# Row transfers in pairs behind a slot's adds, outputs written over fetched rows, and q . bk by ScalarE

## The chip, the cores and the metric

The kernel runs on one core of a Trainium2 chip. The metric is device time in microseconds of one execution; lower is better. Engines are named as in the profile: PE (TensorE), DVE (VectorE), ACT (ScalarE), POOL (GpSimd, which also issues the indirect DMAs) and SP (SyncE, which issues most direct DMAs). Each engine works through its own instructions strictly in order, and waits for others on semaphores.

## The reference

The input is an image batch x of 4 x 256 channels x 64 x 64, in float32. Two layers follow each other.

```python
# layer 0: group norm, then attention over a 3x3 window of every pixel, added to x
x = x + L0_conv(gn(x), Wq, bq, Wk, bk, Wv, bv, Wo, bo)
#   q = (xn @ Wq + bq) * scale; k, v over the padded image; softmax over 9 neighbours; out @ Wo + bo
# layer 1: pixels become 4 x 4096 tokens of 256 values
t = tokens(x)
t = t + L1_attn(ln(t), Wp, bp, Wg)     # gate g = sigmoid(tanh(t Wp + bp) Wg); windowed sum of g*t over 64, divided by that of g
t = t + L1_ffn(ln(t), router_w, w1, b1, w2, b2)
#   out = tokens + sum over the 2 best of 8 experts of weight * (gelu(tokens @ w1[e] + b1[e]) @ w2[e] + b2[e])
x = from_tokens(t)
```

In the last step each of the 16,384 tokens goes through two of eight experts only. The kernel uses that: it sorts token rows by expert, runs each expert on its own rows, and adds the results back to the tokens.

## The kernel before, in words

**Blocks.** The 16,384 pixels are cut into 32 blocks g of 512 (eight per image), and a block into four tiles of 128 tokens. Four generators work on a block, one after the other, each in a later round of the main loop: `produce(g)` normalises x and computes v and q (L455, L459, L481, L485); `attend(g)` makes the 3x3 attention (L535 to L577) and the first token norm, whose reciprocal root is L339 on POOL; `tail(g)` does the gated window sum, stores the token sum to `out` (L685), and leaves the normalised rows in a tile `tok` with each token's eight expert weights and its row number behind the 256 values; `ranks(g)` counts, with two small matmuls, at which row of which expert's region each token stands (`rows`, cast by DVE at L768). In round g of the loop `attend(g)`, `ranks(g - 2)`, `tail(g - 1)` and `produce(g + 1)` take turns.

**Row transfers.** At the end of `ranks` a block's rows are written to HBM (`rows_in`) sorted by expert: four tiles by two choices, so eight indirect DMAs of 128 rows per block, 256 in all, issued by POOL (L783). The helper `paced` makes each wait for the latest marked ACT instruction, so that they are spread out. The inner function `dispatch` declares that transfers don't depend on each other, and records them for the fetches.

**Slots.** A slot is 256 rows of one expert. There are 135. They are grouped: thirteen groups of two blocks, then six of one block (`GROUPS`), and a group's slots can be fetched when all transfers of its blocks have landed. Groups have 1, then twelve times 8, five times 4 and at last 18 slots. For slot m the generator `experts()` emits: `fetch` (SP, L882: 256 rows into a tile sx of the pool `rowp`, of seven buffers), `matrix` (ACT, L899) and `pixels` (PE transposes L906, ACT copy L910) two slots ahead of the output; `hidden` (PE L918, ACT gelu L924) one slot ahead; `output` (PE L936, then DVE L940 adds b2 into a tile ys of three buffers and L941 multiplies by the token's weight), for each of two halves of 128 rows; and `add` one slot behind. A fetch is emitted two slots ahead of its `pixels`, so four ahead of the slot's output.

**Adds.** `add` issues two indirect DMAs on POOL (L954) that add the 128 rows of ys each to `out`, with the row numbers taken from sx. Two slots may add to the same token, so both wait until both adds of the slot before have landed. The first slot of a group also waits for the stores of its blocks.

**Order.** The functions are written in this order, and a scheduler places the instructions of each engine; what is decided once is fixed in the engine's program. `follow` emits slots at an even pace between `knots`, so that the slots of one group run while the blocks of the next are produced. What is left of the slots after the last block runs alone.

**The sums q . bk.** For each block three small POOL instructions (L468, L471, L474) add the constant `qbk` to one column of v and leave `qdotb`, which the softmax of the next round needs (L547).

Of the kernel before, what the change touches and what calls it, by code (L numbers as in the profile page):

```python
# [46 lines left out]
FP = mybir.dt.float32  # L47
AF = mybir.ActivationFunctionType
ALU = mybir.AluOpType
# [3 lines left out]
P = 128  # L53
# [9 lines left out]
def hybrid_block_kernel(ctx: ExitStack, tc: tile.TileContext, ins: dict, out: bass.AP):  # L63
    nc = tc.nc
    x = ins["x"]
    B, C, HW = x.shape
    W = 64
    NC = C // P
    TB = 512
    NT = TB // P  # L70
# [11 lines left out]
    FETCH = 2  # L82
    I32, U32 = mybir.dt.int32, mybir.dt.uint32
    ENG = mybir.EngineType
    GROUPS = (*[2] * 13, *[1] * 6)
    assert sum(GROUPS) == NB
    where = [(k, j) for k, n in enumerate(GROUPS) for j in range(n)]

    U = 2
# [10 lines left out]
    RW = C + 2 * E  # L100
    IN_RANGE = "a slot's expert and row are computed on the chip from counts of a known sum"

    const = ctx.enter_context(tc.tile_pool(name="const", bufs=1))
    xsp = ctx.enter_context(tc.tile_pool(name="xsp", bufs=4))
    xp = ctx.enter_context(tc.tile_pool(name="xp", bufs=XBUFS))
    xtp = ctx.enter_context(tc.tile_pool(name="xtp", bufs=TBUFS))
    vp = ctx.enter_context(tc.tile_pool(name="vp", bufs=3))
# [1 line left out]
    w2p = ctx.enter_context(tc.tile_pool(name="w2p", bufs=2))  # L109
    w3p = ctx.enter_context(tc.tile_pool(name="w3p", bufs=3))  # L110
    w4p = ctx.enter_context(tc.tile_pool(name="w4p", bufs=4))
    slotp = ctx.enter_context(tc.tile_pool(name="slotp", bufs=3))
    rowp = ctx.enter_context(tc.tile_pool(name="rowp", bufs=FETCH + 5))
    w1sp = ctx.enter_context(tc.tile_pool(name="w1sp", bufs=3))
    hbm = ctx.enter_context(tc.tile_pool(name="hbm", bufs=1, space=bass.MemoryType.DRAM))
    ps_a = ctx.enter_context(tc.tile_pool(name="ps_a", bufs=5, space=PSUM))
# [243 lines left out]
    qb = const.tile([P, NC], FP, tag="qb", name="qb")  # L360
    vo = const.tile([P, NC, C + 1], FP, tag="vo", name="vo")
    qbk = const.tile([P, 1], FP, tag="qbk", name="qbk")
    bqb = w2p.tile([P, 2, NC, P], FP, tag="xl_tok", name="bqb")
    for ci in range(NC):
        nc.gpsimd.tensor_copy(bqb[:, 0, ci, :], bq[:, ci : ci + 1].to_broadcast([P, P]))
        nc.gpsimd.tensor_copy(bqb[:, 1, ci, :], bv[:, ci : ci + 1].to_broadcast([P, P]))
# [59 lines left out]
    def produce(g):  # L426
        if g >= NB:
            return
        b, i = divmod(g, NBI)
        if i == 0:  # L430
            image_norm(b)
        mean, rc = norm[b]
        t = xn[g] = xt.pop(g)
        lo = W if i == 0 else 0
        hi = XW - W if i == NBI - 1 else XW
        for c in range(NC):
            tc.keep_in_program_order(nc.vector.tensor_scalar(  # L437
                t[:, c, lo:hi], t[:, c, lo:hi], mean[:, c : c + 1], rc[:, c : c + 1],
                ALU.subtract, ALU.mult,
            ))  # L440
        if lo:
            nc.gpsimd.memset(t[:, :, 0:lo], 0.0)
        if hi < XW:
            nc.gpsimd.memset(t[:, :, hi:XW], 0.0)
        yield


        v = vp.tile([P, NT, C + 1], FP, tag="v", name=f"v_{g}")
        vt[g] = v
        if i == 0:  # L450
            v0[b] = w1p.tile([P, C + 1], FP, tag="v0", name=f"v0_{b}")
        for j in range(0 if i == 0 else 1, NT + 1):
# [12 lines left out]
        qdotb = w2p.tile([P, NT], FP, tag="qdotb", name=f"qdotb_{g}")  # L465
        ct[g] = qdotb
        H = P // 2
        nc.gpsimd.tensor_scalar(  # L468
            qdotb[0:H, 0:1], first[H:P, C : C + 1], qbk[H:P], None, ALU.add
        )  # L470
        nc.gpsimd.tensor_scalar(  # L471
            qdotb[0:H, 1:NT], v[H:P, 0 : NT - 1, C], qbk[H:P], None, ALU.add
        )
        nc.gpsimd.tensor_scalar(qdotb[H:P, :], v[0:H, :, C], qbk[0:H], None, ALU.add)  # L474

        q = w2p.tile([P, NC, TB], FP, tag="q", name=f"q_{g}")
        qt[g] = q
        for co in range(NC):
            ps = ps_a.tile([P, TB], FP, tag="a", name=f"psq_{g}_{co}")
            for ci in range(NC):  # L480
                nc.tensor.matmul(  # L481
                    ps, qk[:, ci, co * P : (co + 1) * P], t[:, ci, W : W + TB],
                    start=(ci == 0), stop=(ci == NC - 1),
                )
            nc.scalar.activation(q[:, co, :], ps, AF.Identity, bias=qb[:, co : co + 1])  # L485
            if co == NC - 1:

                tc.keep_in_program_order(nc.vector.tensor_add(
                    xT[g], xT[g], outb.unsqueeze(1).to_broadcast([P, NT, C])
                ))  # L490
            yield
# [99 lines left out]
    def tail(g):  # L591
# [73 lines left out]
            if t == 1:  # L665
                yield
        mv, rstd = token_norm([t2[:, t, :] for t in range(NT)], f"f{g}", rsqrt_v)
        tok = w2p.tile([P, NT, RW], FP, tag="xl_tok", name=f"tok_{g}")
        for t in range(NT):
            nc.vector.tensor_scalar(  # L670
                tok[:, t, 0:C], t2[:, t, :], mv[:, t, 0:1], rstd[:, t : t + 1],
# [65 lines left out]
    def ranks(g):  # L737
# [26 lines left out]
        nc.vector.tensor_mul(own, hot, row.unsqueeze(1).to_broadcast([P, 2, NT, E]))  # L764
        rowf = w2p.tile([P, 2, NT], FP, tag="rowf", name=f"rowf_{g}")
        nc.vector.tensor_reduce(rowf, own, AX.X, ALU.add)
        rows = w2p.tile([P, 2, NT], U32, tag="rows", name=f"rows_{g}")
        nc.vector.tensor_copy(rows, rowf)  # L768
        yield

        def dispatch(inst):

            for i in range(k + 1):
                tc.declare_no_dep(
                    inst, group=f"dispatch_{i}", reason="no two tokens have one row"
                )
            tc.declare_no_dep(inst, group="fetch", reason="fetched rows are not written again")
            tc.add_to_no_dep_group(f"dispatch_{k}", inst)
            dispatched[k].append(inst)

        for t in range(NT):
            for c in range(2):
                dispatch(paced(nc.gpsimd.indirect_dma_start(  # L783
                    out=rows_in[:, :],
                    out_offset=bass.IndirectOffsetOnAxis(ap=rows[:, c, t : t + 1], axis=0),
                    in_=tok[:, t, :], in_offset=None,
                )).ins)
            yield
        if j < n_blocks - 1:
            return  # L790
# [65 lines left out]

    ready = []
    adds = []

    def experts():  # L860

# [15 lines left out]
        def fetch(m):  # L877
            k = of[m][0]
            assert k in ready
            at = load(m, 1, [ENG.SP], E * ROOM)  # L880
            xs = rowp.tile([P, U, RW], FP, tag="xs", name=f"sx_{m}")
            inst = nc.sync.dma_start(xs, rows_at(at)).ins  # L882
            for i in range(k + 1, len(GROUPS)):
                tc.declare_no_dep(
                    inst, group=f"dispatch_{i}", reason="its rows are of groups up to its own"
                )
            tc.add_to_no_dep_group("fetch", inst)
            for d in dispatched[k]:
                tc.add_manual_dep(
                    inst, d.name,  # L890
                    mybir.DependencyInfo(mybir.DependencyClass.Sync, mybir.DependencyReason.DATA),
                    reason="rows of the slot",
                )
            return xs
# [34 lines left out]

        def output(m, e, h, xs):  # L930
            ps = ps_s.tile([P, U, C], FP, tag="s", name=f"psy_{m}")
            ys = slotp.tile([P, U, C], FP, tag="ys", name=f"ys_{m}")
            done[m] = ys, xs
            for t in range(U):
                for f in range(NC):
                    nc.tensor.matmul(  # L936
                        ps[:, t, :], h[:, f, t * P : (t + 1) * P], w2[:, e, f, :],
                        start=(f == 0), stop=(f == NC - 1),
                    )
                nc.vector.tensor_add(ys[:, t, :], ps[:, t, :], b2b[:, e, :])  # L940
                nc.vector.tensor_scalar_mul(  # L941
                    ys[:, t, :], ys[:, t, :], xs[:, t, bass.ds(e + C, 1)]
                )
                yield

        def add(m, ys, xs):
            k, n = of[m]

            behind = adds[-U:]
# [3 lines left out]
            for t in range(U):  # L953
# [1 line left out]
                    out=out, out_offset=bass.IndirectOffsetOnAxis(  # L955
                        ap=xs[:, t, C + E : C + E + 1].bitcast(U32), axis=0
                    ),
                    in_=ys[:, t, :], in_offset=None, compute_op=ALU.add,
                ).ins
                tc.declare_no_dep(  # L960
                    inst, group="stores", keep=behind, reason="rows of a later group's blocks"
# [4 lines left out]
                for d in behind:  # L966
# [5 lines left out]
                        reason="sums of one row",  # L972
                    )
                tc.add_to_no_dep_group("adds", inst)
                adds.append(inst)

        raw = {m: fetch(m) for m in range(FETCH)}
        xcs, hs, done = {}, {}, {}
        for m in range(-2, total + 1):
            if FETCH <= m + 2 + FETCH < total:  # L980
                raw[m + 2 + FETCH] = fetch(m + 2 + FETCH)
            if m + 2 < total:
                xcs[m + 2] = matrix(m + 2), pixels(m + 2, raw[m + 2])
            yield
            if 0 <= m + 1 < total:
                hs[m + 1] = expert_of(m + 1), hidden(m + 1, *xcs.pop(m + 1))
            yield
            if m > 0:
                add(m - 1, *done.pop(m - 1))
            if 0 <= m < total:  # L990
                yield from output(m, *hs.pop(m), raw.pop(m))

    first_of = [sum(GROUPS[:k]) for k in range(len(GROUPS))]

    for g in range(TBUFS):
        load_xT(g)
# [87 lines left out]
```

## Time and profile before

| what | value |
|---|---|
| median of 3 runs | 1412.79 us (1408.81 to 1413.75) |
| the profiled execution's own time | 1404.04 us |
| its span, first to last instruction | 1402.3 us |
| PE busy | 1271.8 us, 91% of the span |
| DVE, ACT, POOL busy | 989.7, 772.4, 772.5 us |
| adds L954 | 270, mean 1612 ns on POOL |
| row transfers L783 | 256, mean 998 ns on POOL |
| mean granted clock of TensorE | 0.971 |

The page of a profile has busy time by engine, then the span in 40 equal slices of 35 us whose digits are tenths of busy time, then the chain of work that ended last, and groups of instructions: line, engine, operation, output tile <- inputs, shape, count, busy time in us, mean ns of one, and the idle time just before them with what ended most of it. Rows of waits read: who waited <- for whom: us in total, times, the longest. Rows of a timeline: start in us, duration, engine, line, operation, and in square brackets the engine's idle time before it. [...]

### The profile page before, as it was taken

The page shows a single profiled execution, that of the slowest core. Times are in us where ns is not written, and L with a number is a line of the kernel's source. Part 1 is how long each engine was busy: PE and PEld are TensorE (multiplying, and loading weights), DVE is VectorE, ACT ScalarE, POOL GpSimd, SP SyncE. Part 2 cuts the span into 40 slices and gives each one's busy share as a digit, 9 for nine tenths or more (in the row PEclk, how much of TensorE's full clock was granted, in tenths as well). Part 3 has the DMA queues.
Part 4 walks back from the last instruction along what each step waited for, and adds up shares of the span by engine and source line. Part 5 has one row for each costly group of instructions (what it writes and reads, how often), then busy time and mean ns, then how long its engine had stood idle before and what let it go on. Part 6 is the DMA issues. An engine that isn't in the chain of part 4 may idle for free. (4 is left out here: it accounts for less than half of the span.)

```text
span 1402.3 us, 23444 instructions
## 1 busy us (share of the span) xinstructions
PE 1271.8 (91%) x6224; PEld 1053.7 (75%) x6224; DVE 989.7 (71%) x4649; ACT 772.4 (55%) x1509; POOL 772.5 (55%) x711
## 2 busy tenths in 40 slices
PE   5898999999999999999999999999999999777761
PEld 4677777888888877888888878888888888555550
DVE  4599979787877787787878787787867788522221
ACT  1334357766666665676667655666666665323220
POOL 2133535556566666656566556666665666655444
PEclk8999999999999999999999999999999999889896
DMA  9724455555665655565555555555566555565543
GB/s 329 256 96 136 132 168 127 135 148 138 154 149 135 155 128 139 135 166 139 145 131 134 140 138 115 119 140 138 123 136 125 112 110 114 127 146 87 82 70 37
DMA packets 147794, 190.44 MB, mean 136 GB/s; under 512 B 13776, under 2 KB 121936, under 8 KB 147536
## 3 DMA queue, kind: packets, MB, share of 16 engines
q0 software_dynamic: 51168, 71.07, 28.5%
q1 hardware_dynamic: 94000, 116.42, 26.9%
q10 hardware_dynamic: 2496, 1.45, 0.4%
q8 instruction: 52, 0.85, 0.3%
q14 instruction: 78, 0.64, 0.2%
HBM read 98.31 MB, written 90.59 MB: 135 GB/s over the span
## 5 line engine op out<-in xcount | busy, mean ns | idle before, releaser
L954 POOL DMA_INDIRECT out<-ys,sx x270 | 435.2, 1612 | 312.0 <-DVE ys L940 78.5
L936 PE MATMUL psy<-w,h 128*128 x1080 | 290.0, 391 | 74.2 <-DVE ys L940 70.7
L783 POOL DMA_INDIRECT rows_in<-tok,rows x256 | 255.6, 998 | 102.5 <-issue 67.4
L936 PEld LDWEIGHTS psy<-w,h 128*128 128x128 f32 x1080 | 202.9, 193 | 129.2 <-DVE ys L940 95.2
L918 PE MATMUL psh<-xc,w1s 128*128 128x256 f32 x1080 | 269.9, 394 | 0.3 <-DVE ys L940 0.3
L940 DVE TENSOR_TENSOR ys<-psy,b2b 128x256 f32<-128x256 f32 x270 | 113.3, 420 | 178.1 <-DMA out<-ys,sx 104.7
L918 PEld LDWEIGHTS psh<-xc,w1s 128*128 128x128 f32 x1080 | 207.6, 198 | 28.8 <-issue 1.0
L924 ACT ACTIVATE h<-psh,w1s 128x256 f32<-128x256 f32 x270 | 116.6, 477 | 161.5 <-PE psh L918 136.9
L910 ACT COPY xc<-ptx 128x512 f32<-128x512 f32 x135 | 79.5, 589 | 129.0 <-PE ptx L906 79.4
L455 PE MATMUL psv<-vo,x 128*128 128x257 f32 x528 | 128.2, 386 | 12.6 <-DVE x L437 8.9
L481 PE MATMUL psq<-x,qk 128*128 128x512 f32 x256 | 123.6, 592 | 0.0
L535 PE MATMUL pss<-x,q 128*128 128x256 f32 x512 | 122.7, 382 | 0.1
L572 PE MATMUL psc<-v,pT 128*128 128x256 f32 x512 | 121.9, 380 | 0.7 <-issue 0.4
L455 PEld LDWEIGHTS psv<-vo,x 128*128 128x128 f32 x528 | 98.8, 193 | 28.3 <-issue 8.5
L572 PEld LDWEIGHTS psc<-v,pT 128*128 128x128 f32 x512 | 96.4, 189 | 28.8 <-issue 8.4
L535 PEld LDWEIGHTS pss<-x,q 128*128 128x128 f32 x512 | 95.1, 191 | 13.8 <-ACT xc L603 1.0
L941 DVE TENSOR_SCALAR ys<-ys,sx 128x256 f32<-128x256 f32 x270 | 99.8, 370 | 4.5 <-issue 0.2
L924 ACT ACT_TABLE_LOAD x78 | 100.1, 1283 | 1.4
L552 ACT ACTIVATE pe<-logits,stop 128x259 f32<-128x259 f32 x128 | 64.3, 503 | 55.8 <-DVE stop L548 21.4
L576 DVE SCALAR_TENSOR_TENSOR xT<-psc,den,xT 128x256 f32<-128x256 f32 x128 | 55.6, 475 | 51.0 <-PE psc L572 50.2
L471 POOL TENSOR_SCALAR qdotb<-v,qbk 64x3 f32<-64x3 f32 x32 | 12.2, 382 | 140.9 <-ACT v L459 61.6
L603 ACT COPY xc<-ptx 128x512 f32<-128x512 f32 x64 | 35.8, 581 | 96.8 <-PE ptx L600 73.6
(187 smaller groups left out, 2311.0 us busy)
## 6 DMA issues: line engine op xcount, KB each, us to landing
sx<-rows_in SPq DMA_DIRECT2D x135, 272.0 KB
xs<-in_x SPq DMA_DIRECT2D x32, 512.0 KB
xT<-in_xT SPq DMA_DIRECT2D x32, 512.0 KB
out<-xT SPq DMA_DIRECT2D x32, 512.0 KB
x<-in_x SPq DMA_DIRECT2D x24, 640.0 KB
x<-in_x SPq DMA_DIRECT2D x8, 576.0 KB
out<-ys,sx POOLq DMA_INDIRECT x270
rows_in<-tok,rows POOLq DMA_INDIRECT x256
```

Of the source, the lines that this page charges most:

```text
L455: nc.tensor.matmul(ps, t[:, ci, j * P : (j + 1) * P], vo[:, ci, :], start=(ci == 0), stop=(ci == NC - 1),)
L481: nc.tensor.matmul(ps, qk[:, ci, co * P : (co + 1) * P], t[:, ci, W : W + TB], start=(ci == 0), stop=(ci == NC - 1),)
L535: nc.tensor.matmul(ps, q[:, ci, t * P : (t + 1) * P], t_[:, ci, t * P : t * P + NK], start=(ci == 0), stop=(ci == NC - 1),)
L572: nc.tensor.matmul(ps[:, u, :], pT[:, u, j, :], vals[j], start=(j == 0), stop=(j == 1))
L783: dispatch(paced(nc.gpsimd.indirect_dma_start(out=rows_in[:, :], out_offset=bass.IndirectOffsetOnAxis(ap=rows[:, c, t : t + 1], axis=0), i ...
L910: nc.scalar.copy(xc, pt)
L918: nc.tensor.matmul(ps[:, f, :], w1s[:, o : o + P], xc[:, ci, :], start=(ci == 0), stop=(ci == NC - 1),)
L924: inst = nc.scalar.activation(h[:, f, :], ps[:, f, :], AF.Gelu, bias=w1s[:, F1 + f : F1 + f + 1])
L936: nc.tensor.matmul(ps[:, t, :], h[:, f, t * P : (t + 1) * P], w2[:, e, f, :], start=(f == 0), stop=(f == NC - 1),)
L940: nc.vector.tensor_add(ys[:, t, :], ps[:, t, :], b2b[:, e, :])
L941: nc.vector.tensor_scalar_mul(ys[:, t, :], ys[:, t, :], xs[:, t, bass.ds(e + C, 1)])
L954: inst = nc.gpsimd.indirect_dma_start(out=out, out_offset=bass.IndirectOffsetOnAxis(ap=xs[:, t, C + E : C + E + 1].bitcast(U32), axis=0), ...
```

## The change

Row transfers: for the blocks of the first two groups they stay as they are. For every later block `ranks` no longer issues its transfers, but puts them in a list `waiting`. `add` takes two of them out behind each slot's two adds (`give_rows(2)`); `in_turn` fixes the order on POOL between them and the adds without a semaphore. `fetch` first issues what the list still holds of the slot's group (`give_rows(0, k)`). `paced` no longer applies to these. The tiles `tok` and `rows` get three buffers in place of two, since they are held longer; the pool for statistics loads (`xsp`) goes from four to three.

Outputs: the tile ys and its pool are gone. L940 and L941 write into the first 256 columns of the fetched rows sx, which have been transposed by then, and the adds read there. `rowp` goes from seven to nine buffers.

The sums: the three POOL instructions become three ACT instructions with `qbk` as their bias.

```diff
-    xsp = ctx.enter_context(tc.tile_pool(name="xsp", bufs=4))
+    xsp = ctx.enter_context(tc.tile_pool(name="xsp", bufs=3))
...
-    slotp = ctx.enter_context(tc.tile_pool(name="slotp", bufs=3))
-    rowp = ctx.enter_context(tc.tile_pool(name="rowp", bufs=FETCH + 5))
+    rowp = ctx.enter_context(tc.tile_pool(name="rowp", bufs=FETCH + 7))
...
-        nc.gpsimd.tensor_scalar(
-            qdotb[0:H, 0:1], first[H:P, C : C + 1], qbk[H:P], None, ALU.add
-        )
+        nc.scalar.activation(
+            qdotb[0:H, 0:1], first[H:P, C : C + 1], AF.Identity, bias=qbk[H:P]
+        )
...
-        tok = w2p.tile([P, NT, RW], FP, tag="xl_tok", name=f"tok_{g}")
+        tok = w3p.tile([P, NT, RW], FP, tag="xl_tok", name=f"tok_{g}")
...
-        rows = w2p.tile([P, 2, NT], U32, tag="rows", name=f"rows_{g}")
+        rows = w3p.tile([P, 2, NT], U32, tag="rows", name=f"rows_{g}")
...
+        def give(t, c):
+            return nc.gpsimd.indirect_dma_start(
+                out=rows_in[:, :],
+                out_offset=bass.IndirectOffsetOnAxis(ap=rows[:, c, t : t + 1], axis=0),
+                in_=tok[:, t, :], in_offset=None,
+            )
+
         for t in range(NT):
             for c in range(2):
-                dispatch(paced(nc.gpsimd.indirect_dma_start(
...
-                )).ins)
+                if g < first_of[2]:
+                    dispatch(paced(give(t, c)).ins)
+                else:
+                    waiting.append((k, lambda t=t, c=c: in_turn(
+                        dispatch(give(t, c).ins), adds[-1:], given_rows
+                    )))
...
+    waiting, given_rows = [], []
+
+    def in_turn(inst, others, own):
+        for d in others:
+            tc.add_manual_dep(
+                inst, d.name,
+                mybir.DependencyInfo(
+                    mybir.DependencyClass.NoSync, mybir.DependencyReason.SCHED_ONLY
+                ),
+                reason="order of the indirect transfers",
+            )
+        own.append(inst)
+
+    def give_rows(n, k=None):
+        while waiting and (n > 0 or k is not None and waiting[0][0] <= k):
+            waiting.pop(0)[1]()
+            n -= 1
...
             assert k in ready
+            give_rows(0, k)
...
-            ys = slotp.tile([P, U, C], FP, tag="ys", name=f"ys_{m}")
-            done[m] = ys, xs
+
+            ys = xs[:, :, 0:C]
+            done[m] = xs
...
-                    in_=ys[:, t, :], in_offset=None, compute_op=ALU.add,
+                    in_=xs[:, t, 0:C], in_offset=None, compute_op=ALU.add,
...
+                in_turn(inst, given_rows[-2:], [])
                 adds.append(inst)
+            give_rows(2)
```

More of the change, by code (lines that the diff above doesn't have):

```diff
@@ L86, in hybrid_block_kernel @@
     assert sum(GROUPS) == NB
+    first_of = [sum(GROUPS[:k]) for k in range(len(GROUPS))]
     where = [(k, j) for k, n in enumerate(GROUPS) for j in range(n)]
@@ L362, in hybrid_block_kernel @@
     qbk = const.tile([P, 1], FP, tag="qbk", name="qbk")
[L363 removed]
+    bqb = w3p.tile([P, 2, NC, P], FP, tag="xl_tok", name="bqb")
     for ci in range(NC):
@@ L467, in produce @@
         H = P // 2
-        nc.gpsimd.tensor_scalar(
-            qdotb[0:H, 0:1], first[H:P, C : C + 1], qbk[H:P], None, ALU.add
-        )
-        nc.gpsimd.tensor_scalar(
-            qdotb[0:H, 1:NT], v[H:P, 0 : NT - 1, C], qbk[H:P], None, ALU.add
+        nc.scalar.activation(
+            qdotb[0:H, 0:1], first[H:P, C : C + 1], AF.Identity, bias=qbk[H:P]
+        )
+        nc.scalar.activation(
+            qdotb[0:H, 1:NT], v[H:P, 0 : NT - 1, C], AF.Identity, bias=qbk[H:P]
         )
-        nc.gpsimd.tensor_scalar(qdotb[H:P, :], v[0:H, :, C], qbk[0:H], None, ALU.add)
+        nc.scalar.activation(qdotb[H:P, :], v[0:H, :, C], AF.Identity, bias=qbk[0:H])
         q = w2p.tile([P, NC, TB], FP, tag="q", name=f"q_{g}")
@@ L779, in dispatch @@
             dispatched[k].append(inst)
+            return inst
+        def give(t, c):
[4 more added lines that the diff above has]
+            )
         for t in range(NT):
             for c in range(2):
[L783 to L786, printed above, removed]
-                )).ins)
+                if g < first_of[2]:
[4 more added lines that the diff above has]
+                    )))
             yield
@@ L944, in output, with add @@
                 yield
-        def add(m, ys, xs):
+        def add(m, xs):
             k, n = of[m]
@@ L988, in experts @@
             if m > 0:
-                add(m - 1, *done.pop(m - 1))
+                add(m - 1, done.pop(m - 1))
             if 0 <= m < total:
                 yield from output(m, *hs.pop(m), raw.pop(m))
-    first_of = [sum(GROUPS[:k]) for k in range(len(GROUPS))]
     for g in range(TBUFS):
```

## The prediction

> **What bounds the kernel now.** I read the page's busy rows and chain first, then the engines' busy time by stretch, the waits, and last GpSimd's timeline. The profile page:
>
> ```profile
> span 1402.3 us, 23444 instructions
> ...
> PE   5898999999999999999999999999999999777761
> ...
> POOL 2133535556566666656566556666665666655444
> ...
> DMA out<-ys,sx 5%; PE psy L936 1%; DVE ys L940 1%; POOL out L954 1%; DVE ys L941 0%; POOLq L1080 0%; DVEq L940 0%; POOLq L954 0%
> ...
> L954 POOL DMA_INDIRECT out<-ys,sx x270 | 435.2, 1612 | 312.0 <-DVE ys L940 78.5
> ...
> L783 POOL DMA_INDIRECT rows_in<-tok,rows x256 | 255.6, 998 | 102.5 <-issue 67.4
> ```
>
> TensorE is full up to slice 34 (about 1190 us) and never again; the chain that ended last consists of the adds' landings. Busy time by stretch (PE, PEld, DVE, ACT, POOL, clock, DMA) says the same:
>
> ```profile
> 800.00:1000.00 200.00, 196.37 (x984) 163.37 (x984) 154.21 (x739) 130.18 (x245) 121.55 (x106) 1.00 0.56 132
> 1250.00:1300.00 50.00, 34.77 (x152) 28.40 (x151) 11.67 (x30) 15.65 (x32) 23.43 (x16) 0.92 0.52 81
> ```
>
> So there are two regimes. To 1190 us TensorE is the bound (98% busy); after it nothing is busy, and something serial runs. The waits name it:
>
> ```profile
> DVE ys L940 <- DMA out<-ys,sx: 104.7, 25, 5.7
> SPq L882 <- DMA out<-ys,sx: 705.4, 121, 22.9
> ```
>
> Asked for 1190 to 1402 us alone, the first row is again 104.7 us in 25 waits: VectorE waits for landed adds only in the tail. GpSimd's timeline shows the serial step, in the middle and in the tail (start, duration, idle before it):
>
> ```profile
> 730.04 1.65 POOL L954 DMA_INDIRECT out<-ys,sx  x1 [0.28 <-POOL qdotb L468]
> 731.99 1.56 POOL L954 DMA_INDIRECT out<-ys,sx  x1 [0.30 <-DVE xT L488]
> 733.86 1.00 POOL L783 DMA_INDIRECT rows_in<-tok,rows  x1 [0.30 <-issue]
> 735.16 0.98 POOL L783 DMA_INDIRECT rows_in<-tok,rows  x1 [0.31 <-issue]
> 736.57 1.59 POOL L954 DMA_INDIRECT out<-ys,sx  x1 [0.43 <-issue]
> 738.47 0.98 POOL L783 DMA_INDIRECT rows_in<-tok,rows  x1 [0.31 <-issue]
> ...
> 748.24 1.63 POOL L954 DMA_INDIRECT out<-ys,sx  x1 [1.98 <-DVE trstd_f L355]
> ```
>
> ```profile
> 1359.25 1.55 POOL L954 DMA_INDIRECT out<-ys,sx  x1 [3.06 <-DVE ys L940]
> 1361.11 1.56 POOL L954 DMA_INDIRECT out<-ys,sx  x1 [0.30 <-DVE ys L941]
> 1365.71 1.55 POOL L954 DMA_INDIRECT out<-ys,sx  x1 [3.04 <-DVE ys L940]
> ```
>
> A slot's two adds take 1.55 + 0.30 + 1.56, then GpSimd stands about 3.05 us until they have landed: a step of 6.46 us (1359.25 to 1365.71). Two row transfers fit into that gap: 730.04 to 736.57 holds both and is 6.53 us. Where four stand between a slot's adds, the slot takes 11.67 us (736.57 to 748.24), because the landing gap then comes on top.
>
> Numbering the slots 0 to 134 and following their adds in the timeline gives the place where the regimes meet. Up to slot 102 the adds trail the slot's output, mostly by 3 to 9 us, and cost nothing. From there TensorE makes a slot every 6 us (L941 done at 1168.4, 1174.1, 1179.5, 1185.2, 1191.2, 1198.5, 1204.6 for slots 102 to 108), while the adds start at 1169.8, 1177.5, 1184.1, 1193.0, 1199.7, 1211.4, 1217.9. They never catch up: slot 134's first add starts at 1391.6. What the change does to GpSimd's steps from slot 101 (1157.2 us) on sets the end.
>
> **Part 1: transfers two by two.** 256 transfers of 1.00 us with 0.30 before each stay; none is removed. In the order of the changed program's instructions on GpSimd the last blocks' transfers stand in pairs behind slots 101 to 111, and 23 slots follow the last pair (24 before). Steps with a pair in the gap, in this trace: 6.53, 7.18, 6.65, 7.17 (from 730.0, 767.4, 1090.0, 1123.6); mean 6.9. Bare steps of the tail: from 1254.4 (slot 113) to 1391.6 (134), 137.2 / 21 = 6.53, of which I take 6.48, since two (7.25, 6.98) are stragglers. Slots 101 to 111: 11 x 6.9 = 75.9; the L339 behind slot 101 (1.04 + 0.2, in a gap already filled with 2.6 of 3.1) adds 0.7; slots 112 to 133: 22 x 6.48 = 142.6. Sum 219.2 us from slot 101's first add to slot 134's. Before: 1391.6 - 1157.2 = 234.4. Gain 15.2 us. With 6.5 for the paired step it is 19.6, with 7.2 it is 11.9.
>
> The steps keep this pace only if inputs are there. Slot 108's pair, the first of block 31, comes at 1157.2 + 0.7 + 7 x 6.9 + 3.4 = 1209.6; its rows are cast at:
>
> ```profile
> 1203.87 0.16 DVE L768 CAST rows<-rowf 128x8 uint32<-128x8 f32 x1
> ```
>
> 5.7 us of slack. Block 30's (behind slot 104, 1182.0) has rows at 1180.0: 2 us. Outputs come ahead of the adds, 1204.6 against 1206.2 at slot 108, narrowly.
>
> What is late next are the fetches (L882), each group's first behind its own transfers. In a group of two blocks slot i+4's fetch stands behind slot i-2's adds and four forced transfers: 3.4 + 4 x 1.28 + landing 2.7 (a row write ended at 725.98, its waiter L471 began at 728.68) + 4.0 (least time from a fetch's issue to its L906) = 15.2 us. TensorE needs the rows 27.9 us after the output (slot 43's L941 632.2, slot 49's L906 660.1). 12.7 us remain for the adds' own lag, now 4 to 9. The first such group (slot 9) has ten transfers at once: slot 3's output 246.4, + 1.6 + 10 x 1.28 + 2.7 + 4.0 = 267.5, needed at 276.1. Narrowest is slot 109: 1171.7 + 3.4 + 2.6 + 2.7 + 4.0 = 1184.4, needed at 1186.7. On SyncE's queue the loads of x, xT and the statistics stand behind such a fetch; each is for at least one later block (34 us), so I take 0. If the fetch cover is gone, each us late is up to 18 us, once per later group.
>
> **Part 2: outputs in place of rows.** Work is unchanged: 270 L940 (420 ns) and 270 L941 (370 ns) write into sx instead. The wait of L940 for ys buffers (104.7 us) goes, as do TensorE's waits for it (57.0 us after 1190), but both hang on the adds' chain, so alone they give 0. The wait moves to SyncE: a fetch needs the adds of nine slots earlier instead of seven. Worth 0 to the end.
>
> A rule speaks against this part. With the old wait gone, L941 can run at any time during GpSimd's descriptor work. In the tail L941 lies both outside and inside an add:
>
> ```profile
> 1314.61 1.56 POOL L954 DMA_INDIRECT out<-ys,sx  x1 [0.30 <-DVE ys L940]
> 1314.61 0.35 DVE L941 TENSOR_SCALAR ys<-ys,sx 128x256 f32<-128x256 f32 x1
> ```
>
> 1.56 us with L941 inside, 1.55 to 1.56 without. The Trainium skill, "SBUF — State Buffer", section "Who interferes with whom", says that a tensor_scalar on SBUF alone can take a two-port mode that locks GpSimd out for the whole instruction. By the rule 2 x 0.35 us on each of the last 34 slots would be +24 us, and the gain gone; by the row it is 0. I take the row.
>
> **Part 3: the sums by ScalarE.** GpSimd loses 0.42 + 0.38 + 0.33 = 1.13 us per block and the waits in front of them, 141 us at L471 (sixteen times for row transfers); but the last lies at 1123, ahead of slot 101, so the tail gains 0. ScalarE gains 96 activations of 1 to 4 elements with a bias. From L485 (512 elements, 687 ns) and L924 (256, 477) the constant is 267 ns: 0.8 us per block, 26 us in all. They stand just ahead of L485, where ScalarE idles 72.5 us (70.1 for TensorE's psq L481). The table loads are 156 in both programs. I take +1 us; without the cover it is +26.
>
> **Part 4: buffers.** Three for tok and rows let a block's transfers wait. The statistics loads drop from four to three; VectorE waits for them 11.5 us in all, all before 210 us. 0.
>
> **The sum.** 1402.3 - 15.2 + 1 = 1388.1 span. The profiled execution took 1404.04, 1.7 outside the span: 1389.8. The median shown, 1412.79, is 8.75 above the profiled execution: 1398.6, so 1398.
>
> **Rivals.**
> - *Transfers late (slower).* Transfers sit behind adds that wait for outputs, the next group's fetch behind them, TensorE's L906 behind that, and outputs behind L906. It decides at an add lag of 12.7 us; every us beyond costs up to 18. To end 7 us slower it must eat 15 + 7 = 22, a lag of 14. For it: the lag before is already 4 to 9, 15 in the tail; against it: with pairs in the gaps a block costs GpSimd 4.2 x 6.9 + 1.2 = 30 us where TensorE gives 34, so the lag shrinks. At a lag of 15: 2.3 x 18 = 41, so 1398 + 41 = 1439.
> - *ScalarE pays (same).* Half of the 26 us exposed, or the lock in half of the slots: +12, 1410. Against it: between 600 and 800 us the matmuls wait 0.2 us for ScalarE, the weight loads 2.3.
> - *The backlog doesn't shrink.* If slots 102 to 108 lag as now for another reason (outputs late), only the steps behind slot 108 shorten (8.84, 7.03, 7.49 to 6.9): 2.7 us, 1410.
> - *More.* Paired steps at 6.5 give 4.4 more, and TensorE's 21 us idle between 210 and 1200 partly go: 1383.
>
> **How the numbers follow.** A measurement of this kernel can tell about 0.5% (7 us) from no change. Forecast 0.68, its own range 1392 to 1404; late transfers 0.11; ScalarE or lock 0.07, backlog stays 0.06: together 0.13 near 1410; more 0.08. Leaving out the slow case and half of "more", 8 in 10 lie in 1386 to 1412. Faster: 0.68 + 0.08 + a little of the 1410 cases = 0.77; same 0.12; slower 0.11.
>
> **What would show it.** Right: the GpSimd timeline from 1160 has add, add, transfer, transfer with steps near 6.9 and no step of 11; slot 108's first add starts at 1204 to 1210, not 1217.9; no L940 waits for landed adds; PE busy in 800 to 1000 stays near 196. Wrong: L906 idles for sx landings at every group's first slot (it idles 5.6 us in all now); L954 grows beyond 1.61 us; or paired steps of more than 7.6, at which the gain is half.

## The result, and the profile after

The changed kernel takes 1394.38 us (median of 6 runs, 1389.25 to 1398.9), beside 1410.89 us for the kernel before on the same chip (6 runs, 1406.22 to 1413.85). The medians are 16.5 us apart; the ratio, which is not taken from these two medians alone, is 0.9896, with a 95% interval of 0.9866 to 0.9926, so about 1% faster. One caution for all that follows: the profiled execution of the changed kernel took 1398.9 us and was the slowest of its six, while that of the kernel before (1404.04 us) was quicker than all of these six. The two traces show only 5 us of the 16.5, so second executions of both were profiled later.

The page of the changed kernel, rows as before:

```profile
span 1397.2 us, 23159 instructions
...
PE   5898999899999999999999999999999999859740
...
POOL 2023414555665655655666556565655666654444
...
DMA out<-sx 4%; PE psy L967 2%; POOL out L985 2%; PE psh L948 2%; DMA sx<-rows_in 1%; PE ptx L936 0%; DMA rows_in<-tok,rows 0%; DVE sx L971 0%; POOL rows_in L783 0%; POOLq L1111 0%; DVE sx L972 0%; POOLq L985 0%; SPq L912 0%; DVE ends L828 0%; DVE slots L827 0%
...
L985 POOL DMA_INDIRECT out<-sx x270 | 431.1, 1597 | 443.8 <-DVE sx L972 126.8
L783 POOL DMA_INDIRECT rows_in<-tok,rows x256 | 267.3, 1044 | 124.2 <-issue 67.3
```

The adds (now L985) and the row transfers keep their number; an add takes 1597 ns where it took 1612, a row transfer 1044 where it took 998. The chain that ended last still begins with the adds' landings. TensorE's last digits are new: 8, 5, 9, 7, 4, 0 where it was 7, 7, 7, 7, 6, 1. It does the same work earlier in the tail and is done long before the adds. Busy time by stretch:

```profile
800.00:1000.00 200.00, 198.36 (x993) 165.28 (x992) 157.62 (x746) 137.28 (x263) 119.37 (x90) 1.00 0.57 133
1250.00:1300.00 50.00, 47.38 (x227) 39.31 (x226) 17.76 (x45) 21.50 (x44) 23.84 (x16) 0.99 0.54 86
```

TensorE is at 198.4 us of 200 in the middle (196.4 before), and at 47.4 of 50 in the tail (34.8). The waits of the whole execution, with VectorE's first row, then SyncE's fetch:

```profile
DVE sx L971 <- PE psy L967: 127.5, 75, 15.8
...
SPq L912 <- DMA out<-sx: 176.7, 36, 10.4
```

VectorE's wait for landed adds (104.7 us) is gone; it waits for TensorE. The fetches wait for landed adds 176.7 us where it was 705.4. None of this moves the end, which hangs on GpSimd's steps:

```profile
1181.72 1.60 POOL L985 DMA_INDIRECT out<-sx  x1 [2.29 <-DVE pj L626]
1183.62 1.58 POOL L985 DMA_INDIRECT out<-sx  x1 [0.30 <-DVE step L837]
1185.51 1.00 POOL L783 DMA_INDIRECT rows_in<-tok,rows  x1 [0.30 <-DVE first_row L860]
1186.81 0.98 POOL L783 DMA_INDIRECT rows_in<-tok,rows  x1 [0.30 <-issue]
1190.29 1.60 POOL L985 DMA_INDIRECT out<-sx  x1 [2.51 <-DVE tst_f L498]
...
1196.78 1.60 POOL L985 DMA_INDIRECT out<-sx  x1 [0.41 <-DVE nt_f L352]
1198.69 1.57 POOL L985 DMA_INDIRECT out<-sx  x1 [0.30 <-DVE at L706]
1200.56 1.13 POOL L783 DMA_INDIRECT rows_in<-tok,rows  x1 [0.30 <-issue]
1202.00 0.98 POOL L783 DMA_INDIRECT rows_in<-tok,rows  x1 [0.30 <-issue]
1203.29 1.60 POOL L985 DMA_INDIRECT out<-sx  x1 [0.30 <-issue]
```

The order is the one announced: add, add, transfer, transfer. From slot 106 (1196.78) the step is 6.51 us: the pair hides the landing. From slot 104 (1181.72) it is 8.57, because GpSimd still stands 2.51 us after the pair. From slot 101 on the longest steps were 12.51 and 11.73 us; now they are 8 to 9.

The table follows the first adds of slots 101, 112 and 134 through the traces. "Lag" is the mean time from a slot's output (VectorE's multiplication done) to the start of its second add, over slots 6 to 95.

| profiled execution | its time | lag | slot 101 | 101 to 112 | 112 to 134 | slot 134 |
|---|---|---|---|---|---|---|
| before | 1404.0 | 5.7 | 1157.2 | 90.7 | 143.6 | 1391.6 |
| before, second | 1409.1 | 9.8 | 1161.1 | 92.0 | 143.7 | 1396.8 |
| changed | 1398.9 | 0.7 | 1157.7 | 83.3 | 145.7 | 1386.7 |
| changed, second | 1395.3 | 0.8 | 1155.8 | 82.1 | 145.0 | 1383.0 |
| Part 1 alone | 1395.0 | 1.0 | 1156.7 | 82.0 | 144.1 | 1382.7 |
| Part 3 alone | 1398.8 | 1.7 | 1153.4 | 89.9 | 143.1 | 1386.4 |
| changed, seven row buffers | 1391.5 | 0.5 | 1153.5 | 80.4 | 145.3 | 1379.2 |
| Parts 1 and 3 | 1390.7 | 0.6 | 1153.2 | 80.9 | 144.3 | 1378.3 |
| Part 3, sums twice | 1400.0 | 9.1 | 1152.8 | 90.7 | 144.0 | 1387.5 |

So the pairs take 7 to 10 us out of slots 101 to 112 and nothing after them; slot 101 itself comes between 0.5 us later and 5.3 us earlier, depending on which two executions are compared. Runs below were made on three chips; each is compared with the kernel before on its own chip, which took 1409.0 us on the first two and 1401.6 us on the third.

### The profile page after: what moved, and what is told of

Its sections match the earlier page's. It is cut to its first block, busy times and chain, and to the rows that moved or that the text cites. A ratio compares the mean times of both kernels' runs of the same rounds, so it can differ in the third digit from the quotient of the medians.

```text
span 1397.2 us, 23159 instructions
## 1 busy us (share of the span) xinstructions
PE 1262.4 (90%) x6224; PEld 1049.8 (75%) x6224; DVE 988.1 (71%) x4649; ACT 803.6 (58%) x1605; POOL 743.0 (53%) x615
## 5 line engine op out<-in xcount | busy, mean ns | idle before, releaser
L985 POOL DMA_INDIRECT out<-sx x270 | 431.1, 1597 | 443.8 <-DVE sx L972 126.8
L783 POOL DMA_INDIRECT rows_in<-tok,rows x256 | 267.3, 1044 | 124.2 <-issue 67.3
L967 PE MATMUL psy<-w,h 128*128 x1080 | 285.5, 387 | 10.0 <-DVE sx L971 7.2
L948 PE MATMUL psh<-xc,w1s 128*128 128x256 f32 x1080 | 260.5, 383 | 3.8 <-issue 2.8
L971 DVE TENSOR_TENSOR sx<-psy,b2b 128x256 f32<-128x256 f32 x270 | 113.2, 419 | 158.2 <-PE psy L967 127.5
L948 PEld LDWEIGHTS psh<-xc,w1s 128*128 128x128 f32 x1080 | 200.9, 192 | 30.3 <-issue 4.0
L940 ACT COPY xc<-ptx 128x512 f32<-128x512 f32 x135 | 79.6, 590 | 151.7 <-PE ptx L936 106.8
L936 PE MATMUL ptx<-ident,sx 128*128 128x128 f32 x540 | 84.2, 279 | 36.8 <-DMA sx<-rows_in 36.2
L936 PEld LDWEIGHTS ptx<-ident,sx 128*128 128x128 f32 x540 | 67.1, 146 | 57.3 <-issue 39.0
L535 PEld LDWEIGHTS pss<-x,q 128*128 128x128 f32 x512 | 95.8, 192 | 13.6 <-ACT xc L603 0.9
L972 DVE TENSOR_SCALAR sx<-sx 128x256 f32<-128x256 f32 x270 | 99.0, 367 | 4.3 <-issue 0.2
```

What stands on the lines that cost most here:

```text
L535: nc.tensor.matmul(ps, q[:, ci, t * P : (t + 1) * P], t_[:, ci, t * P : t * P + NK], start=(ci == 0), stop=(ci == NC - 1),)
L783: return nc.gpsimd.indirect_dma_start(out=rows_in[:, :], out_offset=bass.IndirectOffsetOnAxis(ap=rows[:, c, t : t + 1], axis=0), in_=tok[: ...
L936: nc.tensor.transpose(pt[:, c, t * P : (t + 1) * P], xs[:, t, c * P : (c + 1) * P], ident)
L948: nc.tensor.matmul(ps[:, f, :], w1s[:, o : o + P], xc[:, ci, :], start=(ci == 0), stop=(ci == NC - 1),)
L967: nc.tensor.matmul(ps[:, t, :], h[:, f, t * P : (t + 1) * P], w2[:, e, f, :], start=(f == 0), stop=(f == NC - 1),)
L972: nc.vector.tensor_scalar_mul(ys[:, t, :], ys[:, t, :], xs[:, t, bass.ds(e + C, 1)])
```

## The experiments

**Each part alone.** Part 1 alone: waiting transfers, pairs, three buffers for tok and rows (and three for the statistics loads), but the tile ys, seven row buffers and GpSimd's sums as before. The central lines, against the kernel before:

```diff
+                    waiting.append((k, lambda t=t, c=c: in_turn(
+                        dispatch(give(t, c).ins), adds[-1:], given_rows
+                    )))
...
+            give_rows(2)
```

> Part 1 alone (transfers in pairs, buffers of tok and rows; outputs still in ys, sums still on GpSimd). My theory, the gain is the pairs': 13 to 16 us below before, near 1395, and slot 112's first add starts by about 1240 instead of 1248. Rival, the outputs in place of rows are needed as well, because VectorE stands in L940 for a ys buffer and holds up the last rows' cast: at most 7 us below before.

Measured: 1396.52 us against 1408.99, ratio 0.9915 (0.9893 to 0.9937), 12.5 us faster. The first add of slot 112 starts at 1238.7. The pairs alone carry most of what the whole change gives.

Part 2 alone, with the nine row buffers that came with it:

```diff
-    rowp = ctx.enter_context(tc.tile_pool(name="rowp", bufs=FETCH + 5))
+    rowp = ctx.enter_context(tc.tile_pool(name="rowp", bufs=FETCH + 7))
...
-            ys = slotp.tile([P, U, C], FP, tag="ys", name=f"ys_{m}")
+            ys = xs[:, :, 0:C]
```

> Part 2 alone (outputs over the fetched rows, nine buffers). My theory: 0, within 3 us of before; the waits of L940 for landed adds are gone from the profile and the tail's step stays 6.4 to 6.5 us. Rival, that wait bounds the tail: 8 us or more below before. Rival from the port rule: slower, adds of more than 1.61 us.

Measured: 1417.98 us against 1408.99, ratio 1.0077 (1.005 to 1.0104): 9 us slower. Expected was nothing.

Part 3 alone (the last of its three sums):

```diff
...
-        nc.gpsimd.tensor_scalar(qdotb[H:P, :], v[0:H, :, C], qbk[0:H], None, ALU.add)
+        nc.scalar.activation(qdotb[H:P, :], v[0:H, :, C], AF.Identity, bias=qbk[0:H])
```

> Part 3 alone (the sums q . bk as activations). My theory: 0 to +2 us against before. Rival, GpSimd's 219 us of qdotb work and waits held up transfers and adds: 5 us or more below before. Rival, ScalarE pays: 8 us or more above.

Measured: 1395.27 us against 1408.99, ratio 0.9907 (0.9886 to 0.9927): 13.7 us faster, where nothing was expected. The lag of the adds fell from 5.7 to 1.7 us.

The change without Part 1 (Parts 2, 3 and 4; transfers where they were):

> The changed kernel with part 1 undone (every transfer issued by ranks, as before; outputs in place, sums on ScalarE, three statistics buffers stay). My theory: within 4 us of before, near 1411. Rival, parts 2 and 3 bring a good share: 7 us or more below before.

Measured: 1398.15 us, ratio 0.9933 (0.991 to 0.9956): 10.8 us faster. The parts don't add up: -12.5, +9 and -13.7 us alone, -16.5 together. Two things had to be found: what Part 3 gives, and what Part 2 or its buffers take.

**What two more row buffers cost.** The changed kernel with seven row buffers, Parts 1 and 3 without Part 2, and the changed kernel again, on one chip.

```diff
-    rowp = ctx.enter_context(tc.tile_pool(name="rowp", bufs=FETCH + 7))
+    rowp = ctx.enter_context(tc.tile_pool(name="rowp", bufs=FETCH + 5))
```

> The changed kernel with seven buffers for a slot's rows in place of nine. Theory that nine buffers let four fetches of 278 KB leave together, which then stand in the way of the adds' landings: slots 104 to 113 step by 6.9 us on average and not 7.5, the first add of slot 112 comes 55 to 57 us after that of slot 104, and the time is 2 to 5 us below the changed kernel's. Rival, the fetches are innocent and the pairs of row transfers themselves stretch the step: the same 59 us and the same time. Rival, seven buffers starve the matmuls of rows in the tail: slower by 2 us or more, with waits of the transposes for a fetch before slot 117 longer than the 13.8 us of the changed kernel.

> Parts 1 and 3 together, without Part 2: the outputs have their own tile of three buffers again and a slot's rows seven buffers. Theory that writing outputs over the rows costs something of its own (+9 us alone): the time falls below that of the changed kernel by 3 to 9 us, 1386 to 1392. Rival, Part 2 costs nothing once the adds are no longer behind a waiting sum on POOL: within 2 us of the changed kernel, 1393 to 1397. Rival, the longer row of buffers is what the pairs need: slower than the changed kernel by over 3 us.

> The changed kernel once more, for a second profiled execution and as the partner of the next two runs. Ratio to the kernel before 0.9896 +- 0.004, some 1395 us. The theory that bursts of fetches stretch the adds' chain: the first add of slot 112 comes 57 to 60 us after that of slot 104 (59.2 in the first profile, against 55.2 = 8 x 6.9), with idle stretches of POOL of 2 us and more behind the same pairs of row transfers. If those stretches were an accident of one execution, it comes after 55 to 56 us.

Measured, against 1409.02 us for the kernel before: changed kernel again 1396.84 (1392.8 to 1399.35), ratio 0.9909 (0.9877 to 0.994); seven buffers 1391.02 (1389.95 to 1391.5), 0.9864 (0.9831 to 0.9897); Parts 1 and 3 without Part 2 1390.86 (1387.1 to 1391.71), 0.9861 (0.9831 to 0.9892). The ranges of the last two don't touch that of the changed kernel beside them. With seven buffers it makes no difference whether the outputs have their own tile: the 6 us belong to the two more buffers. From slot 104 to 112 the first adds are 56.3 and 56.8 us apart, beside 57.8 and 59.2 with nine. SyncE's fetches in the changed kernel, then with seven buffers:

```profile
1181.11 3.72 SPq L912 DMA_DIRECT2D sx<-rows_in  x4
```

```profile
1176.95 7.32 SPq L912 DMA_DIRECT2D sx<-rows_in  x3
```

With nine buffers the four fetches of a group (272 KB each) leave within 3.7 us, since none of them has to wait for a free buffer. They leave while the adds of slot 104 run (1181.72 to 1185.2), and the landing after it is the late one shown above. With seven buffers two leave by 1178.0, as slot 104's adds begin (1177.6), and the third at 1184.3; the same step is undisturbed (GpSimd with seven buffers, slot 105's first add):

```profile
1182.96 1.04 POOL L783 DMA_INDIRECT rows_in<-tok,rows  x1 [0.30 <-issue]
1184.41 1.60 POOL L985 DMA_INDIRECT out<-sx  x1 [0.41 <-DVE sx L972]
```

From slot 104 to 112 this collision is 1 to 3 us of the 6. The rest lies ahead of slot 101 (1153.5 beside 1155.8 and 1157.7); what makes it was not found. The slow steps to slots 109 and 113 (8.65 and 7.88 us) stay with seven buffers. Beside slot 108's adds there leave two fetches, a store of block tokens and the first blank rows; that these make the step long was seen, not tested.

Part 2 alone with seven buffers, on the third chip:

> The kernel before with the outputs written over the rows (Part 2), and seven buffers for the rows as before, not nine. Theory that the loss of 9 us of Part 2 belonged to the two more buffers: the time of the kernel before within 3 us, 1406 to 1412. Rival, writing over the rows costs it: 1415 to 1421 again.

Measured: 1400.43 us against 1401.58, ratio 0.9994 (0.9976 to 1.0013). With seven buffers, writing the outputs over the rows is worth nothing either way, as the prediction had it.

**Where Part 3's gain comes from.** First the sums by VectorE in the kernel before (again the last of three; there are 96 in all, not 78):

```diff
...
-        nc.gpsimd.tensor_scalar(qdotb[H:P, :], v[0:H, :, C], qbk[0:H], None, ALU.add)
+        nc.vector.tensor_scalar(qdotb[H:P, :], v[0:H, :, C], qbk[0:H], None, ALU.add)
```

> The kernel before, with the three sums q . bk of a block by VectorE and not by ScalarE (or GpSimd). Theory that Part 3's gain is GpSimd's: the sums had waited there 3 to 4 us at a time behind the landing of row transfers, with the adds queued behind them, and VectorE's 78 small sums (some 0.1 to 0.3 us each, 8 to 23 us in all, on an engine that is busy for 70% of the span) cost little: the time falls as with ScalarE, 1392 to 1400, and the adds trail their slots by 0.3 to 2 us. Rival, ScalarE itself is what helped, or VectorE has no room: 1405 to 1412, with longer waits of the output matmuls for the additions of the bias.

Measured: 1415.31 us against 1409.02, ratio 1.0048 (1.0032 to 1.0065): slower. This did not test what it was meant to. The adds' lag fell to 1.5 us, as with ScalarE, but the sums stand in VectorE's order and wait there for the copies of v (idle time of VectorE before the sums and the softmax's two small operations on them):

```profile
  ACT v L459: 46.0, 27
```

VectorE, and TensorE behind it, lost more than GpSimd had given: slot 0's output was already 7.1 us later than before, and slot 101's first add came at 1170.5. Here a short lag was worth nothing, since the wait was put on VectorE.

The second test keeps the sums on ScalarE and lets GpSimd compute them once more, into a tile that nothing reads (beside Part 3 alone; one of three):

```diff
+        again = w2p.tile([P, NT], FP, tag="again", name=f"again_{g}")
...
+        nc.gpsimd.tensor_scalar(again[H:P, :], v[0:H, :, C], qbk[0:H], None, ALU.add)
```

> The kernel before with Part 3 (the sums q . bk by ScalarE), and the three sums computed a second time by GpSimd into a tile that nothing reads. ScalarE and the softmax have what Part 3 gave them; GpSimd has its old instructions back, and with them the wait for the landing of the row transfers in front of each block's sum (53.2 us in 17 stretches in the kernel before). Theory that Part 3's gain is the wait on GpSimd that goes: the gain of 13.7 us is lost again, 1405 to 1412, the adds trail their slots by 3 to 9 us as before. Rival, the gain is ScalarE's (the sums reach the softmax sooner): it stays, 1393 to 1398.

Measured: 1400.52 us against 1401.58, ratio 0.9993 (0.9971 to 1.0014). By the medians there is no gain, and the lag is 9.1 us. That speaks for GpSimd, but doesn't prove it. This run and Part 3 alone stood on different chips, and Part 3 without the second sums and with one target was never timed on this one, where the kernel before is itself 7 us quicker. And the trace doesn't show the loss: slot 101's first add starts at 1152.8, beside 1153.4 with Part 3 alone. What is plain is the wait. The kernel before has, in GpSimd's waits from 210 to 1190 us:

```profile
POOL qdotb L471 <- DMA rows_in<-tok,rows: 50.7, 16, 3.9
```

and this experiment, in the same stretch:

```profile
POOL again L479 <- DMA rows_in<-tok,rows: 63.1, 18, 5.0
```

In the trace the second sum of a block waits for the semaphores of mostly five of the eight queues of indirect transfers, whose landings it has no data from. None of the sums on ScalarE carries such a wait, and of the 96 on VectorE two do. In about half of the blocks GpSimd stands so, for 3.2 us on average and at most 3.9 (here 3.5 and 5.0), with adds and transfers queued behind.

**How GpSimd's lag reaches the end.** The kernel before was profiled again:

> The kernel before, for a second profiled execution, since the first (1404.0 us) was quicker than all but a few of its runs: 1404 to 1414 us. If the first was typical in shape, its adds trail their slots by 3 to 9 us in the stretch to 1150 us and step by 6.4 to 6.6 us from slot 104 on but for slots 105 to 108 with their row transfers, and what it is longer by lies in the stretch in which TensorE is the bound.

Measured: 1403.59 us (18 runs, 1397.42 to 1409.13), ratio to itself 1.0012 (0.9995 to 1.0029); the profiled execution took 1409.13 and is the slowest of the 18. It has what the first one lacks. VectorE's waits from 210 to 1190 us:

```profile
DVE tok L729 <- DMA rows_in<-tok,rows: 13.9, 6, 4.8
...
DVE tok L729 <- issue: 5.6, 1, 5.6
```

L729 writes the row numbers into tok. There are two buffers of tok, so it waits until the row transfers of the block two earlier have landed; the profile names these landings for six of the seven waits and nothing ("issue") for the last. In the first execution L729 waits 0.5 us in all. The last of these waits, on VectorE, then GpSimd and TensorE:

```profile
1057.38 0.40 DVE L940 TENSOR_TENSOR ys<-psy,b2b 128x256 f32<-128x256 f32 x1
1063.40 0.18 DVE L729 TENSOR_SCALAR tok<-place 128x32 uint32<-128x32 f32 x1 [5.62 <-issue]
```

```profile
1060.24 0.98 POOL L783 DMA_INDIRECT rows_in<-tok,rows  x1 [0.30 <-issue]
```

```profile
1064.34 3.78 PE L918 MATMUL psh<-xc,w1s 128*128 128x256 f32 x8 [5.17 <-DVE ys L940]
```

The block's last transfer is issued at 1060.24 and ends at 1061.22; VectorE goes on at 1063.40, 2.2 us later; its additions behind L729 are late, and TensorE, which waits for them, stands 5.17 us. Relative to the first execution the outputs fall back by 7.9 us at this place (slots 89 to 91), more than the wait. Most of the rest is the clock: in and behind the idle stretch the granted clock is 0.50, for 10.2 us from 1060.2 on. The eight matmuls of L918 above take 3.78 us; in the first execution they took 1.99:

```profile
1062.69 1.99 PE L918 MATMUL psh<-xc,w1s 128*128 128x256 f32 x8 [0.30 <-DVE ys L940]
```

Busy time of the second execution from 1065 to 1070 us (the third number from the end is the granted clock, which was 1.00 in the first):

```profile
1065.00:1070.00 5.00, 5.00 (x13) 3.98 (x12) 1.42 (x7) 1.83 (x4) 1.85 (x2) 0.50 0.45 77
```

The experiment with the sums twice falls back there by 6.8 us (L729's counterpart waits 9.0 us in all), Part 2 with seven buffers by 8.2 us (20.5 us in all; its profiled execution too was the slowest of its runs); the clock is 0.50 there too, for 6.8 and 10.2 us. None of the traces with the sums on ScalarE only, or with Part 1, has such a wait. So these waits come and go with GpSimd's lag: 0.5 us of VectorE's time at a mean lag of 5.7 us, 9.0 at 9.1, 19.5 at 9.8. What reaches the outputs is another sum: of the second execution's waits the one of 4.8 us (at 713 us, with 3.4 us at a clock of 0.50) set them back by 5.0 us and the last by 7.9, the others by about 2 us at most. How much of it a median execution has is not shown.

**What bounds the tail.** The adds of every other slot go to a second tensor, so that a slot's adds wait for the landing of the slot two before. The sum of the two tensors is left out, and with it half of the experts' results.

```diff
-            behind = adds[-U:]
-            if n == 0:
+            behind = adds[-2 * U : len(adds) - U]
+            if n < 2:
...
-                    out=out, out_offset=bass.IndirectOffsetOnAxis(
+                    out=out if m % 2 == 0 else other[:, :], out_offset=bass.IndirectOffsetOnAxis(
```

> The changed kernel with the adds of every other slot sent to a second tensor in HBM, so that a slot's adds wait for the landing of the slot two before and not of the one before. It leaves out the sum of the two tensors, so half of the experts' results are not in the output: it tells what the wait for one landing costs in the tail, and is no version of the kernel. Theory that the tail is a chain of adds that each wait for the landing before: the step of 6.45 us without a pair falls to GpSimd's own 3.75 us or to what the matmuls of a slot take (4.2 us), and the time to 1315 to 1350. Rival, the tail is bound by the matmuls or the fetches: over 1380.

Measured: 1320.2 us in one run. GpSimd in its tail:

```profile
1239.69 1.54 POOL L987 DMA_INDIRECT out<-sx  x1 [0.85 <-DVE sx L974]
1241.53 1.54 POOL L987 DMA_INDIRECT out<-sx  x1 [0.30 <-issue]
1243.92 1.54 POOL L987 DMA_INDIRECT other<-sx  x1 [0.85 <-DVE sx L974]
```

The step is 4.23 us, and GpSimd waits for VectorE's outputs, no longer for a landing: the step is now the matmuls'. Slots 112 to 134 take 93.2 us instead of 145. The tail is the chain of landings, as the prediction said. In the changed kernel that chain still takes 22 steps of some 6.6 us from slot 112 on.

## Why the prediction was right, and where it was not

- *The time.* Predicted 1398 us, measured 1394.4, inside the range and on the right side. In part that is luck: Part 1's gain was put too high, Part 3's left out and the cost of the row buffers too, and these errors nearly cancel, as far as the next points can tell them apart.
- *Two regimes, and the tail as a chain of landings:* right, shown by the two targets.
- *Part 1, 219.2 us from slot 101 to 134, gain 15.2:* right in kind, too large in size. Measured 229.0 and 227.1 in the two traces (before 234.3 and 235.7), so 5 to 9 us in this stretch; 226.1 with Part 1 alone, 225.7 with seven buffers. The mis-sized term is 11 x 6.9 + 0.7 = 76.6: it measured 83.3 and 82.1, with seven buffers 80.4. The paired step of 6.9 was the mean of four steps between 730 and 1130 us. In the place where it counts, fetches, stores and blank rows leave at the same time, and single steps are 8 to 9 us. The other term, 22 x 6.48 = 142.6, left out the stragglers and measured 145 to 146.
- *The checks of inputs* held, with less room than given. Block 31's row numbers were cast in time:

```profile
1203.40 0.16 DVE L768 CAST rows<-rowf 128x8 uint32<-128x8 f32 x1
```

  Slot 108's first add stood at 1209.84, at the late end of the 1204 to 1210 given. TensorE's waits for rows came, 31.3 us after 1190 in 8 stretches:

```profile
PE ptx L936 <- DMA sx<-rows_in: 31.3, 8, 13.8
```

  They cost nothing: slot 117, behind the longest, was done 13.6 us before its second add.
- *The first group's ten transfers at once* were said to fit with room. Slots from 5 on came 9.8 us later than before in the first trace, and 10 to 12 us later in the other four traces of kernels with pairs and one target, but not with the adds on two targets; so the pairs alone don't cause it. In the changed kernel TensorE, VectorE and ScalarE all have gaps between 258 and 267 us, in and just after the ten transfers (248.9 to 261.4), most of which the profile ascribes to no one. TensorE stands 6.9 us in its gaps, and again the clock adds to that: it is 0.50 for 10.2 us from 261.4 on, and eight matmuls take 3.76 us where they take 1.90 with two targets:

```profile
267.08 3.76 PE L455 MATMUL psv<-vo,x 128*128 128x257 f32 x8 [4.10 <-DVE so_far L757]
```

  All five traces with the delay have such a stretch (6.8 to 10.2 us); the two-target trace has neither. What ties the gaps to the transfers is open. The 10 us were regained by slot 65 or so: from 400 to 1000 us TensorE is idle 3.8 us instead of 10.9.
- *Part 2, worth 0:* right for the outputs themselves (0.9994 with seven buffers), wrong for the nine row buffers that it brought, which cost 6 us. The rule weighed there (the Trainium skill, "SBUF — State Buffer", section "Who interferes with whom") would have made the adds longer; they measured 1597 ns after 1612. In the changed kernel the 64 adds beside which a multiplication ran took 1580 ns on average and the other 206 took 1602, so the row was the better guide here.
- *Part 4, buffers, 0:* open. The third buffer of tok may take away L729's waits, up to 19.5 us of VectorE in one execution, which the trace at hand did not show; but they are gone with two buffers as well where ScalarE alone makes the sums. No run tried the third buffer of tok by itself.
- *Part 3, 0 for the tail and +1:* this is the step that failed. The price was right: ScalarE's 96 activations take 292 to 298 ns each, 28 us in all (estimated 26), and nothing waits for them. The failing sentence, as far as the runs show, is that the adds' lag of 3 to 9 us ahead of slot 102 costs nothing. The 141 us of waits at L471 were seen and set aside because they ended before slot 101. But GpSimd's queue also carries the row transfers, and their landings free tok for VectorE: one late landing set the outputs back by 7.9 us. The question "what is late next" was asked for the fetches and not for tok. Alone, Part 3 is worth 13.7 us by the medians. Of this the first traces show 4 (slot 101 at 1153.4 beside 1157.2), with TensorE's waits for VectorE's L940 down from 13.7 to 9.4 us from 210 to 1190; why these shrink isn't shown, as L729 doesn't wait in either. The lead is there by slot 30, and from slot 0 to slot 30 the second execution of before gains 4.4 us on the first without Part 3 (Part 3 alone gains 5.2). So the traces confirm a cost of the lag, not the 13.7 us; a different order of the instructions, which the edit also brings, was not tested apart from the second sums.
- *Why the parts don't add up.* Parts 1 and 3 both take away the same lag: it is 1.0 us with the first alone, 1.7 with the second, 0.7 with both. So a shared gain, plus the pairs' 7 to 10 us in slots 101 to 112, less 6 for the nine buffers, gives the order of things. It doesn't close as a sum: the shared gain would be 13.7 us by Part 3 alone, 3 to 5 by Part 1 alone (12.5 less the pairs), and 8 to 11 by the two together (18.1 less the pairs). That is not explained.

The better kernel is therefore the changed one with seven row buffers, 1391.0 us, or without Part 2, 1390.9: both beat the change and the kernel before.

## What to carry to other kernels

A queue that lags is not free just because its last item is in time: list every buffer that its transfers hold and the first instruction that overwrites it, and compare the lag with that slack, not only with the end. A bound that is nearly met by one execution may be broken in another, so a second trace is worth its price when the profiled time differs from the median by more than the effect in question. An idle stretch of the bounding engine can cost more than its length: look at the granted clock behind it. More buffers let fetches leave in a burst, here beside a serial chain of small transfers; the count is a term of the sum, not a free choice.

## What the runs showed that had not been expected

- A small sum on GpSimd stood for the landing of row transfers that it has no data from: up to 3.9 us at a time and 53.2 us in 17 stretches in the whole of the kernel before, up to 5.0 us with the sums twice. The same sum on ScalarE stood for none.
- Landings came later beside bursts: in the first trace of the changed kernel the idle time before the next add after a pair was 0.3 to 0.5 us undisturbed and 1.4 to 2.8 us where fetches, stores or blank rows had left beside it.
- The granted clock fell to 0.50 around short idle stretches of TensorE, before the change and after it: between 210 and 1190 us the fourteen traces have 14 such stretches of 3.4 to 10.2 us. Each of them has idle stretches of TensorE, of 0.6 us or more, within the 12 us ahead of it or in it; others as long (1.5 us at 860 us in the first execution of before) have none behind them.
